# A linear-attention block gated by a Hadamard FFN: preparing work on VectorE handed out one operation at a time behind the reads of PSUM

## The chip, the cores and the metric

One Trainium2 chip, one core of it. The metric is device time of one execution in microseconds, the median of three runs. The profile is of one further execution of the same program.

## The reference

All data are fp32. Eight sequences of 512 tokens with 512 features are layer-normalised (without weights). From the normalised tokens two branches are computed and joined: an attention branch `s` and a gating branch `g`; the result is `x + s * silu(g)`. Cut to what matters:

```
xn = layernorm(x)                                   # (8, 512, 512)
q, k, v = xn @ Wq.T + bq, xn @ Wk.T + bk, xn @ Wv.T + bv
kv = cumsum((elu(k) + 1) * v, axis=tokens)
s  = ((elu(q) + 1) * kv * 32**-0.5) @ Wo.T + bo
h  = fwht(xn * SU_ug) / 64                          # Walsh-Hadamard, 512 wide
up, gate = h @ W_up.T * (.. * 64), h @ W_gate.T * (.. * 64)     # 2048 wide
y  = fwht(silu(gate) * up * SU_dp) / 64
g  = silu(y @ W_down.T * (Wscale_dp * 64))
out = x + s * g
```

## The kernel before

**Fast products.** Every matrix product is done with seven block products in place of eight. The blocks are called P1 to P7; tokens and weights are "encoded" into seven combinations each by additions, and the results are summed from three PSUM banks called px, py and pz (three, one and two buffers). `group` and `token_groups` run one such product with tokens on the moving or on the stationary side. What PE leaves in PSUM is read in two ways: snapshots of px by ACT (`snapshot`, `read`), and sums of a snapshot with py or pz by DVE (`output`, L343 in `group` and L418 in `token_groups`). A group has three such sums in `group` and six in `token_groups`. A bank is free for the next product when its sum has been read. In the output projection px is read by DVE too (L414).

**Pairs of sequences.** The sequences are handled in pairs p = 0 to 3. Attention of pair 0, attention of pair 1, the output projection of pair 0 within it, then the FFN of pair 1, then the FFN of pair 0, then pairs 2 and 3 whole. An attention is six groups (k, v, q, twice); the first FFN is sixteen groups of gate and up, and two of down.

**First-pass weights.** Weights are prepared once and kept in DRAM for the later pairs. The first FFN uses gate and up weights with the input's Hadamard transform folded in. `folded_w` makes one such weight in two steps: `butterflies` (four DVE operations, L777 to L780), then `fold` (two pairs of PE products with a Hadamard matrix, ACT copies, and four DVE encodings in `encode_weights`, L187 to L190). From two folded weights `inner_w` makes a second level of seven for the later pairs, with four DVE additions (L276 to L285) and DMA stores. The down weights get their Hadamard transform in `butterflies_down` (one multiplication L818, then for each half of the columns four stages of an addition L763 and a subtraction L764, so 17 instructions a tile), `fold_down` (PE, ACT, a store to `wd_f`) for each of four tiles, and are encoded by `down_w` in eight pieces. `layernorm` of the sequences 2 and 3 (L123 to L130) and their transposes by `transposed` run beside the first attention.

**What sets the order.** Two things. The program text puts PE's products in a hand-made order with `at(place, fn)` and `advance(n)`: a place is one block product, so the products of neighbouring groups interleave. Then a scheduler orders each engine's instructions by a simulation, among those ready by priority; `background(n)` gives the instructions traced within it a priority n behind. The order is fixed when the program is built. The down weights' steps are started by a table, `plan`, that says after how many groups each is traced, as a whole and in the background:

```
for o, (n, a, b) in enumerate(((1, 4, 6), (4, 7, 9), (7, 10, 12), (10, 13, 15))):
    plan.setdefault(n, []).append(lambda o=o: load_down(o, rs))
    plan.setdefault(a, []).append(lambda o=o: rd.update({o: butterflies_down(o, rs)}))
    plan.setdefault(b, []).append(lambda o=o: fold_down(o, rd[o]))
```

`between()`, called at the end of each group, runs what is due. The butterflies of folded weights are placed 12 places after they are asked for and their fold 6 later, both in the foreground. `get_w` fetches weights for three groups ahead. Weight tiles have four buffers ("w"), working tiles six ("t"), token inputs one ("x"). All these DMAs are issued on SP's queue.

Of the kernel before, what the change touches and what calls it, by code (L numbers as in the profile page):

```python
# [21 lines left out]
def kernel(  # L22
# [27 lines left out]
    nc = tc.nc  # L50
# [32 lines left out]

    cols_sb = const.tile([P, cols.shape[1]], F32, tag="cols", name="cols_sb")
# [13 lines left out]
    wsc_r = const.tile([P, P], F32, tag="wsc_r", name="wsc_r")  # L98
# [17 lines left out]

    def layernorm(b, xt, parts=1):
        n = NT // parts
        for i in range(0, NT, n):
            mv = small.tile([P, n, 2], F32, tag="mv", name=f"mv_{b}_{i}")  # L120
            for t in range(n):
                st = small.tile([P, 6], F32, tag="st", name=f"st_{b}_{i}_{t}")
                nc.vector.bn_stats(st, xt[:, i + t, :])  # L123
                nc.vector.bn_aggr(mv[:, t, :], st)
            rstd = small.tile([P, n], F32, tag="rstd", name=f"rstd_{b}_{i}")
            nc.vector.tensor_scalar(rstd, mv[:, :, 1], EPS, None, ALU.add)
            nc.scalar.activation(rstd, rstd, AF.Sqrt)
            nc.vector.reciprocal(rstd, rstd)
            for t in range(n):
                nc.vector.tensor_scalar(  # L130
                    xt[:, i + t, :], xt[:, i + t, :], mv[:, t, 0:1], rstd[:, t : t + 1],
                    ALU.subtract, ALU.mult,
                )
# [51 lines left out]
    def encode_weights(eng, w):  # L185
        w = w.rearrange("p j s e -> p s j e") if len(w.shape) == 4 else w
        eng.tensor_tensor(w[:, P5], w[:, P7], w[:, P4], ALU.add)  # L187
        eng.tensor_tensor(w[:, P6], w[:, P5], w[:, P1], ALU.subtract)  # L188
        eng.tensor_tensor(w[:, P3], w[:, P2], w[:, P6], ALU.subtract)
        eng.tensor_tensor(w[:, P7], w[:, P1], w[:, P7], ALU.subtract)  # L190

# [59 lines left out]
    def down_w(u, j):  # L251

        t = t8.tile([P, 2, 7, P], F32, tag="t", name=f"wd_{u}_{j}")
        w = by_factor(t)
        rows_w(w, wd_f, u + NU * j, NG)

        def encode():
            encode_weights(nc.vector, w)
            nc.sync.dma_start(wd[u // 2][:, :, 2 * (u % 2) + j], w)

        at(8, encode)

    def inner_w(m, u, w0, w1):

        if u not in inner:
            inner[u] = dram.tile([P, 7, 2, 7, P], F32, tag=f"d_gu_{u}", name=f"d_gu_{u}")
        d = inner[u][:, :, ("gate", "up").index(m)]

        def store(c, t):
            nc.sync.dma_start(d[:, :, c, :], t)  # L270

        store(P1, w0[:, 0])
        store(P2, w0[:, 1])
        store(P4, w1[:, 1])
        t = xin.tile([P, 3, 7, P], F32, tag="x", name=f"s_{m}_{u}")
        nc.vector.tensor_tensor(t[:, 0], w1[:, 0], w1[:, 1], ALU.add)  # L276
        store(P5, t[:, 0])
        nc.vector.tensor_tensor(t[:, 1], t[:, 0], w0[:, 0], ALU.subtract)
        store(P6, t[:, 1])
        nc.vector.tensor_tensor(t[:, 2], w0[:, 1], t[:, 1], ALU.subtract)  # L280
        store(P3, t[:, 2])

        def s3():
            with background():
                nc.vector.tensor_tensor(t[:, 0], w0[:, 0], w1[:, 0], ALU.subtract)  # L285
                store(P7, t[:, 0])

        at(7, s3)
# [27 lines left out]
    def group(name, ws, rhs, dst, at_x, then, bias=(None, None)):  # L316
# [25 lines left out]
        def output(i, s, p):  # L342
            nc.vector.tensor_tensor(dst[i], s, p.rearrange("p a t -> p (a t)"), ALU.add)  # L343
# [41 lines left out]
        between()  # L385


    def token_groups(name, n, tok, wts, dst, add=None, early=None, done=None):
# [28 lines left out]
        def output(o, p, a, s, g):  # L417
            nc.vector.tensor_tensor(dst(a, s, g), o, p, ALU.add)  # L418
            if done:
                done(a, s, g)  # L420
# [55 lines left out]
        between()  # L476
# [64 lines left out]
    def attention(p, xo, get_w, behind):  # L541
# [4 lines left out]
        def project(m, g, then):  # L546
            w = get_w(m, g)
            r = t8.tile([P, 2, 2, L], F32, tag="t", name=f"{m}_{p}_{g}")
            b = (col("b" + m, g), col("b" + m, g + 2))

            def whole(px):
                nc.scalar.activation(r[:, 0, 1], px, AF.Identity, bias=b[0])  # L552

            group(
                f"{m}_{p}_{g}", [w[:, 0], w[:, 1]], x_rhs(xo),
                (r[:, 0, 0], r[:, 1, 0], r[:, 1, 1]), whole, lambda: then(r), b,
            )
            behind.get(next(n), lambda: None)()
# [56 lines left out]
    def project_out(p, co, get_w):  # L615
        ws = [get_w("o", k) for k in range(2)]
        r = [t8.tile([P, NT, D], F32, tag="t", name=f"o_{p}_{s}") for s in range(2)]

        def bias(a, s, g):
            return bo_r[:, a * 2 * P : (a + 1) * 2 * P].unsqueeze(1).to_broadcast([P, 2, 2 * P])  # L620

        token_groups(
            f"o_{p}", 2, lambda k, i: co[:, k, i, :], lambda i: lambda k: ws[k][:, i],
            lambda a, s, g: block(r[s], a, g), bias,
        )
        for s in range(2):
            put_by(f"s_{p}_{s}", r[s])


    def gate(p, f, xo, get_w):  # L630
# [6 lines left out]
        def with_gate():  # L637
# [5 lines left out]
            (g[:, 0, 0], g[:, 1, 0], g[:, 1, 1]), at_x, with_gate,  # L643
# [3 lines left out]
    def up(p, f, g, xo, ho, get_w):  # L647
# [7 lines left out]
        def with_up():  # L655
# [6 lines left out]
            (r[:, 0, 0], r[:, 1, 0], r[:, 1, 1]), at_x, with_up,  # L662
# [58 lines left out]
    def down(p, half, hos, get_w, ds=None, ss=None, ys=None):  # L721
# [21 lines left out]
        def at_ds(a, s, g):  # L743
# [3 lines left out]
            f"dn_{p}_{half}", 4, lambda k, i: hos[k // 2][:, k % 2, i, :], wts, at_ds,  # L747
# [12 lines left out]
    def butterfly(eng, dst, src, h):  # L760
        s = src.rearrange("p (a t h) e -> p a t h e", t=2, h=h)
        d = dst.rearrange("p (a t h) e -> p a t h e", t=2, h=h)
        eng.tensor_tensor(d[:, :, 0], s[:, :, 0], s[:, :, 1], ALU.add)  # L763
        eng.tensor_tensor(d[:, :, 1], s[:, :, 0], s[:, :, 1], ALU.subtract)  # L764

    def folded_w(name, src, f):
# [3 lines left out]
        rs = []  # L770

        def butterflies():
# [4 lines left out]
            nc.vector.tensor_tensor(r2[:, 0], a, b, ALU.add)  # L777
            nc.vector.tensor_tensor(r2[:, 1], a, b, ALU.subtract)
            nc.vector.tensor_tensor(r[:, :, 0], r2[:, :, 0], r2[:, :, 1], ALU.add)
            nc.vector.tensor_tensor(r[:, :, 1], r2[:, :, 0], r2[:, :, 1], ALU.subtract)  # L780

        def fold():
            for b in range(2):
# [11 lines left out]
            encode_weights(nc.vector, w)  # L795
            folded[name, f] = w
            if f >= NU:
                with background():
                    inner_w(name, f - NU, folded[name, f - NU], w)

        return w, [(12, butterflies), (6, fold)]
# [4 lines left out]
    def down_tiles(rs):  # L806
        n = NF * P
        r = [rs[:, i * n : (i + 1) * n].rearrange("p (c e) -> p c e", c=NF) for i in range(2)]
        return r + [rs[:, 2 * n : 2 * n + n // 2].rearrange("p (c e) -> p c e", c=NF)]

    def load_down(o, rs):
        r = rs[o % 2]
        nc.sync.dma_start(r, wdown_t[:, o * P : (o + 1) * P].rearrange("(c p) e -> p c e", p=P))
        nc.sync.dma_start(wsc_r, wscale_dp[o * P : (o + 1) * P].partition_broadcast(P))

    def butterflies_down(o, rs):
        r, r2 = rs[o % 2], rs[2]
        nc.vector.tensor_tensor(r, r, wsc_r.unsqueeze(1).to_broadcast([P, NF, P]), ALU.mult)  # L818
        for e in range(2):
            half = r[:, :, e * P // 2 : (e + 1) * P // 2]  # L820
            butterfly(nc.vector, r2, half, 8)
            butterfly(nc.vector, half, r2, 4)
            butterfly(nc.vector, r2, half, 2)
            butterfly(nc.vector, half, r2, 1)
        return r
# [19 lines left out]
    def first_w(m, g):  # L845
# [18 lines left out]
        return w, [(5, encode)]  # L864

    def later_w(m, g):
        return stream_w((m, g)), []
# [32 lines left out]
    def ask(n):  # L900
        while queue and len(ahead) < n:
            first, m, g = queue.pop(0)
            w, steps = (first_w if first else later_w)(m, g)
            ahead.append({"key": (m, g), "w": w, "steps": steps, "traced": 0, "asked": 0, "place": 0})
# [8 lines left out]
    def get_w(m, g):  # L913
# [4 lines left out]
        for _ in e["steps"]:  # L918
            step_of(e)()
        for i, e in enumerate(ahead):  # L920
# [36 lines left out]
    rd = {}  # L957
    groups = [0]
    plan = {}
    for o, (n, a, b) in enumerate(((1, 4, 6), (4, 7, 9), (7, 10, 12), (10, 13, 15))):  # L960
        plan.setdefault(n, []).append(lambda o=o: load_down(o, rs))
        plan.setdefault(a, []).append(lambda o=o: rd.update({o: butterflies_down(o, rs)}))
        plan.setdefault(b, []).append(lambda o=o: fold_down(o, rd[o]))
    for n, u, j in ((16, 0, 0), (16, 0, 1), (17, 1, 0), (18, 1, 1), (22, 2, 0), (23, 2, 1), (24, 3, 0), (25, 3, 1)):
        plan.setdefault(n, []).append(lambda u=u, j=j: down_w(u, j))

    def between():
        for step in plan.pop(groups[0], []):
            with background():
                step()  # L970
        groups[0] += 1

    def tokens(b, xo):
        t = load_x(b)
        layernorm(b, t)
        transposed(b, t, xo)
# [63 lines left out]
    def next_tokens(b):  # L1040
        with background(40):
            tokens(b, x1)

    co0 = attention(0, x0, get_w, {0: lambda: next_tokens(2), 2: lambda: next_tokens(3), 4: put_x0})
    co1 = attention(1, x1, get_w, {1: lambda: project_out(0, co0, get_w)})
    ffn(1, x1, None, True, co1, {3: fetch_x0})
# [62 lines left out]
```

## Time and profile before

| | |
|---|---|
| median of 3 runs | 1607.16 us (1606.34 to 1608.49) |
| profiled execution | 1607.51 us, span 1605.7 us, mean granted PE clock 0.995 |
| PE busy | 1548.8 us (96% of the span), 5936 matmuls |
| DVE busy | 959.9 us (60%), 1385 instructions |
| ACT busy | 422.2 us (26%) |
| POOL busy | 494.1 us (31%) |
| DMA | 261.64 MB, mean 163 GB/s |

The span is the time from the first to the last instruction; the execution's own time holds a little more at both ends. Busy time counts instructions that run; matmuls are pipelined and their ends are modelled, so PE at 96% is not PE at its peak. In the chain of work that ended last PE has 76%, DVE 12%, POOL 5%. The rows of the timeline name the tile written and the tiles read: `q<-sb_q,pz_q` is the sum of the snapshot sb_q and the bank pz_q into q.

### The profile page before, as it was taken

The page shows a single profiled execution, that of the slowest core. Times are in us where ns is not written, and L with a number is a line of the kernel's source. Part 1 is how long each engine was busy: PE and PEld are TensorE (multiplying, and loading weights), DVE is VectorE, ACT ScalarE, POOL GpSimd, SP SyncE. Part 2 cuts the span into 40 slices and gives each one's busy share as a digit, 9 for nine tenths or more (in the row PEclk, how much of TensorE's full clock was granted, in tenths as well). Part 3 has the DMA queues.
Part 4 walks back from the last instruction along what each step waited for, and adds up shares of the span by engine and source line. Part 5 has one row for each costly group of instructions (what it writes and reads, how often), then busy time and mean ns, then how long its engine had stood idle before and what let it go on. Part 6 is the DMA issues. An engine that isn't in the chain of part 4 may idle for free.

```text
span 1605.7 us, 15724 instructions
## 1 busy us (share of the span) xinstructions
PE 1548.8 (96%) x5936; PEld 1114.4 (69%) x5936; DVE 959.9 (60%) x1385; ACT 422.2 (26%) x677; POOL 494.1 (31%) x286
## 2 busy tenths in 40 slices
PE   6898988999999999999999999999999999999998
PEld 3346435546744688888886468888887468888887
DVE  6896487582377566715684575634675376542673
ACT  2442444231233112111222431111221451111211
POOL 4343121223013425502622236201622128120731
PEclk9999999999999999999999999999999999999999
DMA  8512443684594864335563133525464133525462
GB/s 321 179 62 99 146 134 97 199 274 134 190 277 141 302 236 160 110 114 189 177 251 140 69 125 109 190 93 186 167 256 157 50 113 136 176 84 190 142 258 85
DMA packets 148876, 261.64 MB, mean 163 GB/s; under 512 B 7360, under 2 KB 109248, under 8 KB 144576
## 3 DMA queue, kind: packets, MB, share of 16 engines
q1 hardware_dynamic: 148512, 260.34, 48.0%
q8 instruction: 47, 0.77, 0.2%
q10 hardware_dynamic: 288, 0.30, 0.1%
q14 instruction: 29, 0.24, 0.0%
HBM read 187.20 MB, written 73.40 MB: 162 GB/s over the span
## 4 chain that ended last, share of the span: by engine, by line
PE 76%; DVE 12%; POOL 5%; issue 3%; ACT 2%; DMA 2%; POOLq 0%; SPq 0%; ACTq 0%; DVEq 0%
PE px_gu L487 17%; PE px_dn L403 9%; PE pz_gu L487 9%; PE pz_dn L403 5%; PE py_gu L487 4%; PE px_up L327 3%; PE px_gate L327 3%; PE px_o L403 3%; PE py_dn L403 3%; PE px_k L327 2%; PE px_v L327 2%; PE px_q L327 2%; POOL s L730 2%; PE pz_o L403 2%; PE pz_up L327 1%
## 5 line engine op out<-in xcount | busy, mean ns | idle before, releaser
L403 PE MATMUL px_dn<-w_down,ho 128*128 128x256 f32 x1024 | 229.7, 379 | 2.1 <-DVE sb_dn L414 1.1
L403 PEld LDWEIGHTS px_dn<-w_down,ho 128*128 128x128 f32 x1024 | 193.8, 190 | 31.8 <-DVE sb_dn L414 1.9
L487 PE MATMUL px_gu<-xi,w_gu 128*128 128x256 f32 x672 | 173.3, 380 | 1.2 <-ACT sa_gu L495 1.0
L487 PE MATMUL px_gu<-xo,w_gu 128*128 128x256 f32 x672 | 172.4, 379 | 0.0
L693 POOL TENSOR_TENSOR u<-u,v 128x1024 f32<-128x1024 f32 x24 | 56.2, 2364 | 328.2 <-DVE u L525 295.7
L487 PEld LDWEIGHTS px_gu<-xi,w_gu 128*128 128x128 f32 x672 | 126.9, 190 | 23.2 <-issue 2.4
L487 PEld LDWEIGHTS px_gu<-xo,w_gu 128*128 128x128 f32 x672 | 127.7, 190 | 18.2 <-issue 1.0
L403 PE MATMUL pz_dn<-w_down,ho 128*128 128x256 f32 x512 | 116.8, 380 | 4.0 <-POOL ho L182 4.0
L403 PEld LDWEIGHTS pz_dn<-w_down,ho 128*128 128x128 f32 x512 | 96.5, 190 | 20.1 <-POOL ho L182 4.8
L730 POOL TENSOR_TENSOR s<-s,d 128x512 f32<-128x512 f32 x30 | 41.4, 1379 | 165.0 <-ACT d L728 165.0
L487 PE MATMUL pz_gu<-xo,w_gu 128*128 128x256 f32 x336 | 86.8, 381 | 0.7 <-DVE v L343 0.7
L487 PE MATMUL pz_gu<-xi,w_gu 128*128 128x256 f32 x336 | 86.3, 379 | 0.0
L487 PE MATMUL py_gu<-xo,w_gu 128*128 128x256 f32 x336 | 86.2, 379 | 0.0
L577 POOL TENSOR_TENSOR v<-v,k 128x1024 f32<-128x1024 f32 x16 | 42.2, 2635 | 141.3 <-ACT v L552 90.7
L487 PEld LDWEIGHTS pz_gu<-xo,w_gu 128*128 128x128 f32 x336 | 63.3, 190 | 11.2 <-DVE v L343 1.5
L487 PEld LDWEIGHTS pz_gu<-xi,w_gu 128*128 128x128 f32 x336 | 63.8, 190 | 9.0 <-DVE u L518 0.4
L487 PEld LDWEIGHTS py_gu<-xo,w_gu 128*128 128x128 f32 x336 | 63.8, 190 | 8.7
L697 POOL TENSOR_TENSOR v<-v,r 128x1024 f32<-128x1024 f32 x24 | 56.2, 2362 | 25.6 <-DVE r L525 23.4
L327 PE MATMUL px_gate<-xo,w_gate 128*128 128x512 f32 x128 | 60.3, 599 | 3.7 <-DVE w_gate L188 3.7
L179 POOL TENSOR_TENSOR co<-co 128x512 f32<-128x512 f32 x8 | 15.3, 1918 | 156.9 <-DVE co L587 144.9
L327 PE MATMUL px_k<-xo,w_k 128*128 128x512 f32 x128 | 60.9, 594 | 1.7 <-ACT sa_k L339 1.7
L327 PE MATMUL px_q<-xo,w_q 128*128 128x512 f32 x128 | 61.5, 599 | 0.0
(245 smaller groups left out, 2687.3 us busy)
## 6 DMA issues: line engine op xcount, KB each, us to landing
w_gu<-d_gu SPq DMA_DIRECT2D x84, 896.0 KB, 4.4
w_down<-d_down SPq DMA_DIRECT2D x56, 512.0 KB, 3.4
d_s<-o SPq DMA_DIRECT2D x8, 1024.0 KB, 5.5
d_d<-dn SPq DMA_DIRECT2D x8, 1024.0 KB, 7.4
d<-d_d SPq DMA_DIRECT2D x8, 1024.0 KB, 5.4
s<-d_s SPq DMA_DIRECT2D x8, 1024.0 KB, 7.1
y<-in_x_dram SPq DMA_DIRECT2D x8, 1024.0 KB, 8.5
out_dram<-y SPq DMA_DIRECT2D x16, 512.0 KB, 3.1
```

The costliest lines, as they stand in the source:

```text
L179: eng.tensor_tensor(o[..., P5, :], o[..., P7, :], o[..., P1, :], ALU.subtract)
L327: nc.tensor.matmul(p.rearrange("p a t -> p (a t)") if len(r.shape) == 2 else p, ws[k][:, i, :], r, start=(first and k == 0), stop=(k == n ...
L403: nc.tensor.matmul(p[:, c], t[:, (2 * g + c) * P : (2 * g + c + 1) * P], ws[i](k), start=(first and k == 0 and c == 0), stop=(k == n - 1), ...
L487: nc.tensor.matmul(p[:, lane], w[:, lane, i, :], x(i), start=(first and lane == 0), stop=True, skip_group_check=True,)
L577: nc.gpsimd.tensor_tensor(v[:, h], v[:, h], k[:, h], ALU.mult)
L693: nc.gpsimd.tensor_tensor(r[:, m], ru1[:, m], rv[:, m], ALU.add)
L697: nc.gpsimd.tensor_tensor(rv[:, m], rv[:, m], rr[:, m], ALU.add)
L730: (nc.vector if last else nc.gpsimd).tensor_tensor(r, r, d, ALU.mult)
```

## The change

DVE's preparing operations are no longer traced as whole steps. Each becomes an entry of a list, with a cost in us that the author gives it, in one of two queues: `urgent` (butterflies, encodings and inner weights of gate and up) and `idle` (layernorm of sequences 2 and 3, the down weights' butterflies and encodings). Each sum at L343 and L418 calls `pace` with a budget `us`, and `pace` takes entries from `urgent`, then from `idle`, until the budget is used up. What an entry traces on DVE is queued behind that sum by `tc.issue_after` (an order of issue, without a wait for its end) and has background priority. The budgets are 2.0 in attention, 2.2 in the output projection, 3.2 in gate and up, 3.0 in down. `finish` runs at once what is left of a list when its result is wanted. The table `plan`, `between` and `butterflies_down` go. The operations themselves and their shapes stay, but for the multiplication L818, which is done in two halves, and the order of the four inner weights, which begins with P7. The scale vector of the down weights gets a second buffer; the first two down tiles are loaded after the first group, each further one after the fold two tiles before it. A fold of a down tile is placed 4 places after its last butterfly, in the foreground. The encodings of the down weights for the first half follow the last fold, those for the second half the group down_0.

```diff
+    urgent, idle = [], []
+    def run(step):
+        fn, step[1] = step[1], None
+        if fn:
+            fn()
+    def finish(steps):
+        for step in steps:
+            run(step)
+    def pace(ins, us):
+        while us > 0 and (urgent or idle):
+            step = (urgent or idle).pop(0)
+            if step[1]:
+                with tc.issue_after(ins.ins), background():
+                    run(step)
+                us -= step[0]
...
+    def layernorm_steps(b, xt, tiles=range(NT)):
...
+        return steps_of(
+            *[(0.8, lambda i=i: stats(i)) for i in range(n)], (0.2, root),
+            *[(0.6, lambda i=i: scaled(i)) for i in range(n)],
+        )
...
+    def encode_steps(w):
...
+            *[(0.42, lambda a=a, b=b, c=c, op=op: nc.vector.tensor_tensor(w[:, a], w[:, b], w[:, c], op))
...
     def down_w(u, j):
-        def encode():
-            encode_weights(nc.vector, w)
+        def kept():
             nc.sync.dma_start(wd[u // 2][:, :, 2 * (u % 2) + j], w)
-        at(8, encode)
+        return encode_steps(w) + steps_of((0, kept))
...
     def inner_w(m, u, w0, w1):
...
+        return steps_of(
+            (1.1, lambda: factor(P7, 0, lambda t: w0[:, 0], lambda t: w1[:, 0], ALU.subtract)),
+            (1.1, lambda: factor(P5, 1, lambda t: w1[:, 0], lambda t: w1[:, 1], ALU.add)),
+            (1.1, lambda: factor(P6, 2, lambda t: t[:, 1], lambda t: w0[:, 0], ALU.subtract)),
+            (1.1, lambda: factor(P3, 0, lambda t: w0[:, 1], lambda t: t[:, 2], ALU.subtract)),
+        )
...
         def output(i, s, p):
-            nc.vector.tensor_tensor(dst[i], s, p.rearrange("p a t -> p (a t)"), ALU.add)
+            pace(nc.vector.tensor_tensor(dst[i], s, p.rearrange("p a t -> p (a t)"), ALU.add), us)
...
         advance(7 * u)
-        between()
...
     def folded_w(name, src, f):
         def butterflies():
...
+            rs.extend(steps_of(*[
+                (0.68, lambda x=x: nc.vector.tensor_tensor(*x)) for x in (
...
+            urgent.extend(rs[1:])
         def fold():
+            finish(rs[1:])
...
-            encode_weights(nc.vector, w)
+            enc.extend(encode_steps(w))
+            urgent.extend(enc)
             folded[name, f] = w
             if f >= NU:
-                with background():
-                    inner_w(name, f - NU, folded[name, f - NU], w)
-        return w, [(12, butterflies), (6, fold)]
+                urgent.append([0, lambda: urgent.extend(inner_w(name, f - NU, folded[name, f - NU], w))])
+        return w, [(10, butterflies), (5, fold)], enc
...
+    def down_steps(o, rs):
...
+        def folded():
+            fold_down(o, r)
+            if o + 2 < KD:
+                load_down(o + 2, rs)
+            if o == KD - 1:
+                prepare_down(0)
+        return steps_of(
+            *[(1.2 if op[3] == ALU.mult else 0.68, lambda op=op: nc.vector.tensor_tensor(*op)) for op in ops],
+            (0, lambda: at(4, folded)),
+        )
...
     def later_w(m, g):
-        return stream_w((m, g)), []
+        if m == "down":
+            while not ready[g[0]]:
+                run(idle.pop(0))
+        return stream_w((m, g)), [], []
...
     def get_w(m, g):
...
         for _ in e["steps"]:
             step_of(e)()
+        finish(e["last"])
...
+    def begin(n):
+        if n == 0:
+            next_tokens(2)
+            for o in range(2):
+                load_down(o, rs)
+            for o in range(KD):
+                idle.extend(down_steps(o, rs))
+        elif n == 2:
+            finish(held[2])
+            next_tokens(3)
+        elif n == 4:
+            put_x0()
...
-    ffn(1, x1, None, True, co1, {3: fetch_x0})
+    ffn(1, x1, None, True, co1, {1: lambda: prepare_down(1), 3: fetch_x0})
+    finish(urgent + idle)
```

## The prediction

> **What bounds the kernel now.** I read the page first (the busy rows in forty slices), then the busy time of each engine by stages, then what TensorE waited for in the disturbed stretch, then the timeline of DVE at the longest of these waits. The page:
>
> ```profile
> span 1605.7 us, 15724 instructions
> ...
> PE   6898988999999999999999999999999999999998
> ...
> DVE  6896487582377566715684575634675376542673
> ```
>
> PE stands at 9 from slice 9 on; what it loses it loses before 320 us, where DVE swings between 2 and 9. Columns of the next view: stretch, its length, then busy us of PE, PEld, DVE, ACT, POOL, granted clock, DMA.
>
> ```profile
> 40.00:80.00 40.00, 34.76 (x91) 15.48 (x90) 33.17 (x39) 17.11 (x22) 14.51 (x10) 0.97 0.57 179
> 80.00:120.00 40.00, 39.16 (x98) 17.22 (x97) 37.58 (x53) 18.66 (x26) 17.08 (x10) 0.95 0.18 60
> 120.00:160.00 40.00, 34.22 (x132) 24.34 (x131) 27.11 (x31) 8.65 (x10) 15.28 (x10) 1.00 0.27 96
> 160.00:200.00 40.00, 40.00 (x96) 17.92 (x96) 15.94 (x17) 18.66 (x34) 5.73 (x3) 1.00 0.47 153
> 200.00:240.00 40.00, 32.58 (x74) 13.18 (x73) 32.91 (x39) 16.16 (x36) 8.80 (x4) 1.00 0.43 134
> 240.00:280.00 40.00, 33.16 (x101) 19.85 (x100) 29.68 (x44) 17.35 (x32) 6.35 (x4) 0.91 0.33 98
> 320.00:360.00 40.00, 40.00 (x95) 17.76 (x94) 33.87 (x57) 13.74 (x26) 9.04 (x6) 1.00 0.88 279
> ```
>
> DVE is full in 40 to 120, nearly idle in 160 to 200 and loaded again in 200 to 280. The preparing work comes in lumps. At 320 to 360 a DVE load of 34 of 40 us costs PE nothing, so the load as such is bearable where it is spread. PE's waits from 30 to 310 us:
>
> ```profile
> PE pz_v L327 <- DVE rstd L126: 5.0, 1, 5.0
> PE pwd L831 <- ACT rd L837: 3.9, 3, 3.2
> PE px_gate L327 <- DVE w_gate L188: 3.7, 1, 3.7
> PE pz_q L327 <- DVE q L343: 2.5, 1, 2.5
> PE pz_o L403 <- POOL co L182: 2.4, 1, 2.4
> PE pz_v L327 <- DVE q L343: 2.3, 1, 2.3
> ```
>
> With the smaller ones (1.6, 1.2, 1.0, 0.9, 0.8, 0.7, 0.2) they make 26.2 us. The reduced clock adds 0.03 x 40 + 0.05 x 40 + 0.09 x 40 = 6.8 us. So 33.0 us are lost here. I sort them: 11.5 before 125 us (5.0 + 2.3 + 1.0 and 3.2 of clock); 3.3 in the first output projection at 130 to 155 (1.6 + 0.9 + 0.8), where DVE runs next to no preparing work; 18.2 from 200 to 310. How a wait comes about is seen in DVE's timeline at the first:
>
> ```profile
> 61.63 2.83 DVE L764 TENSOR_TENSOR rd<-rd 128x512 f32<-128x512 f32 x1
> 64.39 2.81 DVE L579 TENSOR_TENSOR_SCAN k<-ones,v 128x512 f32<-128x512 f32 x2
> 67.13 1.15 DVE L763 TENSOR_TENSOR rd<-rd 128x512 f32<-128x512 f32 x1
> 68.20 1.21 DVE L764 TENSOR_TENSOR rd<-rd 128x512 f32<-128x512 f32 x1
> 69.34 2.81 DVE L818 TENSOR_TENSOR rd<-rd,wsc_r 128x2048 f32<-128x2048 f32 x1
> ...
> 77.71 0.67 DVE L343 TENSOR_TENSOR q<-sb_q,pz_q 128x512 f32<-128x512 f32 x1
> ```
>
> From 61 to 77.7 us eight-odd preparing operations on rd and x stand ahead of the reads at L343. The read of pz_q ends at 78.4, and the next product into a pz bank starts at 78.52. No wait was missed by DVE: it is behind with its queue.
>
> **The change, part by part.** The operations stay the same ones: butterflies (L777 to 780), encodings (L187 to 190), inner weights (L276 to 285), layernorm (L123 to 130), the down weights' butterflies (L763, L764, L818). What changes is their place. Each is now queued behind one read at L343 or L418, 2.0 us of them per read in attention, 2.2 in the output projection, 3.2 in gate and up, 3.0 in down.
>
> Attention first. The queue called idle holds two layernorms, each 4 x 0.69 + 0.3 + 4 x 0.5 = 5.1 us, and four down tiles, each 16 adds at 0.605 (start to start) and two half-size multiplications at 1.15 (half of L818's 2.29), 12.0 us: 58 us in all. The transposed tokens' own DVE work adds 6 (the L157 to L162 rows of 40 to 120). At 2.0 us of budget a read takes three adds, so a tile takes six reads and both layernorms seven: 31 reads. Three come per group of attention and six in the output projection, so idle lasts about ten group lengths from 32 us on. A group is 28 matmuls at 0.43 = 12.0 us of PE, so with the transposes this is 124 us of PE work. DVE's own part there is 5.7 us a group (in 40 to 120, five groups: 15 reads x 0.6, 8 scans x 1.2, 8 operations L565 and L587 x 1.21), nine times, and 14 reads x 0.6 of the projection: 59.
>
> **A rule against the change.** The row: L764 at 61.63 takes 2.83 us where 0.68 is usual, while POOL's L577 runs from 61.19 to 63.92. In 40 to 120 the excess over the usual durations is 5.3 (L764), 1.0 (L763), 1.1 (L818), 2.5 (L579), 0.9 (L130), 10.8 us in 80, against POOL's 31.6 busy. The Trainium skill (SBUF — State Buffer, SBUF: two separate sides) says that VectorE with two SBUF inputs and GpSimd take the shared ports as an exclusive lock for a whole instruction. A step between two reads that meets a POOL operation would then hold the next read for all of it, and spreading the steps makes such meetings likelier. By the trace's share, 0.135 x 124 = 16 us, demand on DVE is 59 + 64 + 16 = 139. By the rule at its worst, all of POOL's 46.9 us in 40 to 160, scaled to 48, demand is 171. I take the trace's 16, since it was measured at the same density of steps. The overrun is 139 - 124, less some 4 us that PSUM's banks absorb (the same sum for the old order in 54 to 125 gives 28 + 36 + 11 = 75 in 71 us elapsed): 11 us of PE waiting, where 11.5 + 3.3 = 14.8 were lost. Gain 3.8. So the lumps go, but the average stays near full.
>
> After attention. Before, two down tiles (24 us) lay in DVE's 62.6 busy us of 200 to 280; they are now done by about 165 us, and 38 of 80 us remain. Gone are then most of the pz_q waits (3.2), the px_gate wait (an encoding behind eight adds of rd, 3.7), the pwd wait (ACT waited for a late g, 3.9 and 0.2), the output projection's waits (2.4 and 1.2, late L587) and 3.6 of clock: 18.2. I leave 4 us of it for what the POOL collisions and the folds still cost. Gain 14.2.
>
> On the clock, the row: after the 5.0 us wait, four pz_v matmuls take 3.75 us where 1.88 is usual. The skill (TensorE: Matmul & The Clock Gate, Part 1) lets an idle window of about 3.4 us halve the clock. Here a 3.2 us wait at 240 also cost clock, so the measurement decides. Counting waits alone the part within reach is 22.9 us, with the clock 29.7. I use the latter. Waits split into pieces under 2 us, as the pace leaves them, kept 1.00 in 120 to 160.
>
> Costed at nothing, with the cover named:
> - Two loads of 1 MB (load_down 0 and 1, before at 45.8 and 55.7 us) move ahead to about 22 us on SP's queue, past the weight loads. The next weight load issues at 43.84, waiting for a buffer, so 20 us cover 2 x 6.6 (the landing seen at 231). Without cover up to 13.
> - The folds move with their tile's last step, four matmuls and sixteen ACT copies each, now in the foreground, and with them the stores to wd_f and the loads of tiles 2 and 3, which wait on SP for those stores. Before, DVE waited 2.0 for such a load. Between a gain of 4 and a loss of 5 I take 0, near the row at 168 to 179, four folds with no PE wait.
> - The four first down_w come earlier and each holds one of six "t" buffers from load to store. Before, four did so at 300 to 330 with no PE wait: 0, at worst 2.5 each, 10.
> - Inner weights begin with P7, and P3 waits for P7's store (before, DVE waited 3.4 once for it, no PE wait): 0, at worst 8 x 2.
> - The queue called urgent: a folded weight needs four butterflies at 0.68 and four encodings at 0.42, 4.4 us, every second one also four inner weights at 1.09, 8.8; the budget of a gate or up group is 3 x 3.2 = 9.6, so it drains: 0. That the encodings lose their foreground place is rival 3.
> - The Sqrt between layernorm steps: before 3.5 us passed from L126 to L128 with reads in between: 0.
>
> After 320 us PE has almost no waits and the DVE load is the old one: 0. Sum: 1607.51 (the profiled execution; span 1605.7, 1.8 around it, and 0.35 above the median) - 3.8 - 14.2 = 1589.5; I say 1590.
>
> **The rivals.**
> 1. All waits in reach go: no overrun, since DVE begins at 32 us rather than 54. 29.7 us less, 1578. For it: 160 to 200 was nearly empty. Against: the 139 above.
> 2. The ports decide, slower. Place: 32 to 165 us, POOL's L577 and its encodings against tied steps. At the full 48 us the overrun is 171 - 124 - 4 = 43 instead of 14.8, +28, less 14.2: 1621. It becomes slower when collisions pass 34 us, 70% of POOL's time instead of the 34% seen. Against it: that share was measured with DVE full.
> 3. Weights come late, slower. A background encoding waits for a read to pass before PE may use the weight; the row is px_gate's 3.7 us. At eight of the sixteen folded weights it is 30 us: 1619; from five on (18 / 3.7) the gain is gone. Against: the steps are first in line and are finished when the weight is fetched.
> 4. The edges bind little. They only set an earliest place; the scheduler may pile steps up later as before, and 40 to 120 and 200 to 280 stay full: 1604, gain of the earlier start alone.
>
> **How the numbers follow.** A run here can tell 0.2%, 3.2 us, from no change. Likeliest case 0.48 (its own range 1581 to 1599), rival 1 0.10, rival 2 0.12, rival 3 0.14, rival 4 0.16. Faster: 0.48 + 0.10 + half of rival 4, 0.08 = 0.66. Same: the other 0.08 of rival 4 and 0.04 of rivals 2 and 3 in mild form, 0.12. Slower: 0.22. The range 1577 to 1615 leaves out about half of rivals 2 and 3 above and a little of rival 1 below.
>
> **What would show it.** Right: DVE's digits level between 32 and 320 us, rd's adds done by about 170, no wait of PE over 3 us there, clock 1.00 from 40 on. The three reads' gaps hold at most three adds. Wrong: waits of PE for L343 adding to over 20 us in 32 to 165 (rival 2, with L763 and L764 means over 1 us), for w_gate or w_up (rival 3), or DVE's order unchanged (rival 4).

## The result: slower by half a per cent, and the profile after

Measured beside the kernel before: 1615.33 us (median of 4, 1614.76 to 1616.48) against 1607.36 us, a ratio of 1.005 with a 95% interval from 1.0033 to 1.0068. The forecast was 1590 us, with a range from 1577 to 1615. The page of the changed kernel, the rows that were shown of before (PE is TensorE, PEld its weight loads, DVE VectorE, ACT ScalarE, POOL GpSimd):

```profile
span 1613.7 us, 15738 instructions
...
PE   6988999999999999999999999999999999999998
...
DVE  5899666561467376625675476634675376552673
```

At this grain little has changed. The stages show more (columns as before: stretch, length, busy PE, PEld, DVE, ACT, POOL, granted clock, DMA share, GB/s):

```profile
40.00:80.00 40.00, 37.05 (x107) 18.00 (x106) 33.56 (x59) 20.06 (x29) 13.29 (x10) 0.96 0.53 189
80.00:120.00 40.00, 34.84 (x77) 15.09 (x76) 38.21 (x40) 16.90 (x33) 14.92 (x8) 0.91 0.27 81
120.00:160.00 40.00, 34.70 (x108) 21.04 (x107) 36.10 (x43) 15.38 (x29) 20.32 (x12) 0.96 0.45 150
160.00:200.00 40.00, 37.80 (x112) 20.73 (x111) 27.72 (x44) 12.72 (x38) 2.74 (x1) 1.00 0.68 231
200.00:240.00 40.00, 38.20 (x89) 16.48 (x89) 27.63 (x35) 20.87 (x30) 12.50 (x6) 1.00 0.48 156
240.00:280.00 40.00, 39.98 (x138) 25.64 (x137) 25.73 (x37) 14.80 (x19) 5.92 (x4) 1.00 0.43 122
...
400.00:440.00 40.00, 36.69 (x125) 23.86 (x124) 13.88 (x26) 8.77 (x17) 0.00 (x0) 0.96 0.43 136
...
480.00:520.00 40.00, 32.81 (x69) 13.96 (x69) 31.35 (x36) 11.05 (x22) 15.19 (x9) 0.91 0.50 150
```

Behind 160 us the load of DVE is levelled as intended: 27.7 in 160 to 200 where 15.9 stood, 25.7 in 240 to 280 where 29.7 stood, and PE loses next to nothing from 240 to 280. From 120 to 160 it rose, to 36.1 of 40 us where 27.1 stood. And there are two new holes in PE's work, at 400 to 440 and 480 to 520, in a stage where PE had been full. In the first of them DVE is at 13.9 of 40 us, which is no overload.

Lines of the changed kernel: the sums that read PSUM are L386 and L460 (L343 and L418 before), the butterflies of gate and up L813, their encodings L231, the inner weights L322, the down weights' butterflies L880, layernorm's last step L158. PE's waits by what they waited for, first from 30 to 330 us, then from 320 to 620, the largest of each:

```profile
PE pwd L898 <- DVE rd L880: 5.2, 1, 5.2
PE pt L184 <- DVE x L158: 3.0, 1, 3.0
PE py_o L445 <- DVE o L460: 2.4, 1, 2.4
PE pwd L898 <- issue: 2.0, 1, 2.0
PE pw_gate L826 <- DVE r_gate L813: 1.8, 1, 1.8
PE pwd L898 <- ACT rd L904: 1.7, 1, 1.7
```

```profile
PE pw_gate L826 <- DVE r_gate L813: 6.5, 2, 3.3
PE px_gate L370 <- DVE w_gate L231: 4.0, 1, 4.0
PE pz_dn L445 <- POOL ho L217: 3.2, 2, 1.6
PE pw_up L826 <- DVE r_up L813: 2.1, 2, 1.4
```

The attention products' waits for banks of PSUM (pz_v, pz_q, pz_k before) are gone; in the output projection py_o still waits 2.4 us for its bank. PE now waits mostly in its small products, the Hadamard folds pwd, pw_gate, pw_up and the transposes pt, and for the most part for paced steps; once, at px_gate, it waits for a paced encoding. Adding up each whole list (and the reduced clock, 40 us times what is missing to 1.00 in each stretch) gives the balance:

| PE's waits + clock, us | before | after |
|---|---|---|
| 30 to 320 us | 26.4 + 6.8 | 17.5 + 6.8 |
| 320 to 620 us | 5.3 + 0 | 17.6 + 5.2 |

So 8.9 us are gained and 17.5 lost, 8.6 net, against 8.0 between the spans (1613.7 and 1605.7).

### The profile page after: what moved, and what is told of

Its sections match the earlier page's. It is cut to its first block, busy times and chain, and to the rows that moved or that the text cites. A ratio compares the mean times of both kernels' runs of the same rounds, so it can differ in the third digit from the quotient of the medians.

```text
span 1613.7 us, 15738 instructions
## 1 busy us (share of the span) xinstructions
PE 1554.1 (96%) x5936; PEld 1118.5 (69%) x5936; DVE 949.3 (59%) x1389; ACT 421.5 (26%) x677; POOL 506.1 (31%) x286
## 4 chain that ended last, share of the span: by engine, by line
PE 75%; DVE 13%; POOL 4%; issue 3%; ACT 3%; DMA 2%; SPq 0%; POOLq 0%; DVEq 0%; ACTq 0%
PE px_gu L528 17%; PE px_dn L445 9%; PE pz_gu L528 9%; PE pz_dn L445 4%; PE py_gu L528 4%; PE px_gate L370 3%; PE px_o L445 3%; PE py_dn L445 3%; PE px_k L370 2%; PE px_up L370 2%; PE px_v L370 2%; PE px_q L370 2%; DVE rd L880 2%; POOL s L771 2%; PE pz_o L445 2%
## 5 line engine op out<-in xcount | busy, mean ns | idle before, releaser
L528 PEld LDWEIGHTS px_gu<-xo,w_gu 128*128 128x128 f32 x672 | 127.7, 190 | 18.2 <-issue 1.0
L697 POOL TENSOR_TENSOR ho<-g,u 128x512 f32<-128x512 f32 x8 | 16.0, 2002 | 164.0 <-DVE u L386 164.0
L880 DVE TENSOR_TENSOR rd<-rd 128x512 f32<-128x512 f32 (+1 forms) x72 | 63.0, 898 | 0.6
L214 POOL TENSOR_TENSOR co<-co 128x512 f32<-128x512 f32 x8 | 18.6, 2324 | 141.7 <-DVE co L628 141.7
```

The lines of the kernel that those rows point to most:

```text
L214: eng.tensor_tensor(o[..., P5, :], o[..., P7, :], o[..., P1, :], ALU.subtract)
L528: nc.tensor.matmul(p[:, lane], w[:, lane, i, :], x(i), start=(first and lane == 0), stop=True, skip_group_check=True,)
L697: nc.gpsimd.tensor_tensor(ho[:, P1], g[:, 0, 0], r[:, 0, 0], ALU.mult)
L880: *[(1.2 if op[3] == ALU.mult else 0.68, lambda op=op: nc.vector.tensor_tensor(*op)) for op in ops],
```

## The experiments

Two theories. A step is tied when it is queued behind a read by `tc.issue_after`. Theory 1: a tied step cannot run until its read has run; where that read comes late, and the product that needs the step stands right behind in PE's queue, PE waits for read and steps together. Theory 2: DVE is simply slower or fuller with the steps spread, by POOL's hold on the ports or by load.

What the first hole looks like in DVE's timeline of the changed kernel, with PE's below it:

```profile
402.05 0.69 DVE L460 TENSOR_TENSOR dn<-sc_dn,pz_dn 128x512 f32<-128x512 f32 x1 [6.77 <-ACT sc_dn L454]
405.50 0.69 DVE L460 TENSOR_TENSOR dn<-sc_dn,pz_dn 128x512 f32<-128x512 f32 x1 [2.76 <-ACT sc_dn L454]
415.24 0.69 DVE L460 TENSOR_TENSOR dn<-sb_dn,pz_dn 128x512 f32<-128x512 f32 x1 [9.05 <-PE pz_dn L445]
418.69 0.69 DVE L460 TENSOR_TENSOR dn<-sb_dn,pz_dn 128x512 f32<-128x512 f32 x1 [2.76 <-PE pz_dn L445]
419.30 1.29 DVE L813 TENSOR_TENSOR r_gate<-w_gate 128x512 f32<-128x512 f32 x2
420.62 1.29 DVE L813 TENSOR_TENSOR r_gate<-r_gate 128x512 f32<-128x512 f32 x2
```

```profile
411.59 7.07 PE L445 MATMUL pz_dn<-w_down,ho 128*128 128x256 f32 x32
421.97 3.17 PE L826 MATMUL pw_gate<-r_gate,had 128*128 128x512 f32 x4 [3.31 <-DVE r_gate L813]
424.93 2.44 PE L370 MATMUL px_gate<-xo,w_gate 128*128 128x512 f32 x4
```

DVE idles 9.05 us, then 2.76, and only behind the last read of the down group come the four butterflies, 2.6 us. PE's next product in line is the one that needs them: read 0.6 and butterflies 2.6 are the 3.3 us of the wait. The row of pw_gate shows a second price: its four products take 3.17 us where 1.88 is usual; the granted clock of 400 to 440 is 0.96, which is 1.6 us.

The second hole looks different:

```profile
478.99 2.57 DVE L322 TENSOR_TENSOR s_up<-w_up,w_up 128x896 f32<-128x896 f32 x1
481.49 1.74 DVE L813 TENSOR_TENSOR r_gate<-r_gate 128x512 f32<-128x512 f32 x1
...
485.24 3.42 DVE L813 TENSOR_TENSOR r_gate<-w_gate 128x512 f32<-128x512 f32 x2
488.58 2.57 DVE L231 TENSOR_TENSOR w_gate<-w_gate 128x256 f32<-128x256 f32 x1
```

```profile
483.28 3.04 PE L826 MATMUL pw_gate<-r_gate,had 128*128 128x512 f32 x4 [3.22 <-DVE r_gate L813]
...
494.36 3.62 PE L370 MATMUL px_gate<-xo,w_gate 128*128 128x512 f32 x4 [3.97 <-DVE w_gate L231]
```

From 475.4 to 498 us DVE works without a pause. The last of four butterflies stands behind three reads and two inner weights, the encoding behind the next weight's butterflies; beside POOL's operations an inner weight takes 2.57 us where 1.09 is usual, a butterfly 1.74 where 0.68 is, an encoding 2.57 where 0.42 is. That is a full queue with slowed operations, as theory 2 has it. This hole is the larger one: 3.2 + 4.0 us of waits and 3.6 of clock, against 3.3 + 1.6 of the first.

### a1: the butterflies of gate and up free again

```diff
-            urgent.extend(rs[1:])
+            finish(rs[1:])
```

> The changed kernel, but the four butterflies of each folded gate or up weight are issued at once where they are asked for (not behind a read, foreground), as before the change. Theory 1 (a Hadamard product stands in PE's queue before its butterflies, which are held back behind a late read): PE's waits for r_gate and r_up, 10.4 us together, go, and with them the 5.2 us of reduced clock between 400 and 520 us and most of the 4.0 us wait for w_gate; about 1600 us (1597 to 1604). Theory 2 (DVE is slower as a whole there, by POOL's port or by load, whatever the order): the waits turn up at other reads, 1611 to 1616.

Measured 1598.81 us, ratio to before 0.9953 (0.994 to 0.9965), 16.5 us under the changed kernel. In the same place DVE now does:

```profile
401.86 0.69 DVE L460 TENSOR_TENSOR dn<-sc_dn,pz_dn 128x512 f32<-128x512 f32 x1 [6.77 <-ACT sc_dn L454]
402.46 1.29 DVE L813 TENSOR_TENSOR r_gate<-w_gate 128x512 f32<-128x512 f32 x2
403.78 1.29 DVE L813 TENSOR_TENSOR r_gate<-r_gate 128x512 f32<-128x512 f32 x2
...
415.05 0.69 DVE L460 TENSOR_TENSOR dn<-sb_dn,pz_dn 128x512 f32<-128x512 f32 x1 [3.74 <-PE pz_dn L445]
418.50 0.69 DVE L460 TENSOR_TENSOR dn<-sb_dn,pz_dn 128x512 f32<-128x512 f32 x1 [2.77 <-PE pz_dn L445]
```

```profile
411.40 7.07 PE L445 MATMUL pz_dn<-w_down,ho 128*128 128x256 f32 x32
418.31 1.88 PE L826 MATMUL pw_gate<-r_gate,had 128*128 128x512 f32 x4
```

The butterflies ran some 17 us earlier, in time in which DVE had nothing else, and pw_gate follows at once at its usual pace. From 320 to 620 us PE's waits are 5.2 us, about the 5.3 of before, and no clock is lost: both holes are gone. At the place of the second, DVE's operations are as slow as they were (at 494.79 us two butterflies take 3.42), but they run ahead of need and PE does not wait. Theory 1 forecast the size; under theory 2 the waits would have turned up at other reads, and they did not. Before 320 us the waits are the 17.5 of the changed kernel. The edit lifts the tie and the background priority together; a2 and b2 take these apart.

### a4: half of the change, layernorm and the down weights alone

```diff
-            urgent.extend(rs[1:])
+            finish(rs[1:])
...
-            enc.extend(encode_steps(w))
-            urgent.extend(enc)
+            encode_weights(nc.vector, w)
...
-                urgent.append([0, lambda: urgent.extend(inner_w(name, f - NU, folded[name, f - NU], w))])
+                with background():
+                    finish(inner_w(name, f - NU, folded[name, f - NU], w))
-        return w, [(10, butterflies), (5, fold)], enc
+        return w, [(12, butterflies), (6, fold)], enc
```

> Half of the change: layernorm and the down weights are paced behind reads, gate and up weights (butterflies, encodings, inner weights) are treated as before the change. Theory 1 says that all loss after 320 us comes from the half left out: after 320 us the kernel loses no more than before the change, and before 320 us it keeps the 8.7 us gained; 1597 to 1602. Theory 2: the paced half fills DVE in attention, no gain: 1606 to 1610.

Measured 1598.02 us, ratio 0.9955 (0.9941 to 0.9968): within the runs of a1. So of the gate and up weights it is the pacing of the butterflies that costs; whether their encodings and inner weights are paced is worth nothing here.

### a2: the steps traced at the same reads, without the tie

```diff
-                with tc.issue_after(ins.ins), background():
+                with background():
```

> The changed kernel without the tie: steps are traced one by one at the same reads and in the background, but the scheduler may issue them ahead of the read. Theory 1: the wait of 3.3 us at 420 us, where DVE idles 9 us ahead of the read, goes, and part of the others; 1603 to 1610. If instead the late place in the text and the background priority do the harm and the tie nothing, or under theory 2: 1613 to 1617.

Measured 1605.95 us, ratio 0.9997 (0.9988 to 1.0005). From 320 to 620 us PE waits 5.4 us in place of 17.6 and loses 1.6 us of clock in place of 5.2; from 30 to 320 it waits 23.0 in place of 17.5 and loses 10.4 us of clock in place of 6.8, with the old sort of wait again (`pz_k` for `v`, 4.6 us in one piece). One edge has both effects: it protects the reads in attention and delays the butterflies later.

### b2: tied, but not in the background

```diff
+            behind = 0 if urgent else 150
             step = (urgent or idle).pop(0)
             if step[1]:
-                with tc.issue_after(ins.ins), background():
+                with tc.issue_after(ins.ins), background(behind):
```

> The changed kernel with the steps of gate and up weights still tied behind reads, but without the background priority (those of layernorm and the down weights keep it). If the tie itself is the cause, the late read stands ahead of the butterflies as before and the 3.3 us waits at the Hadamard products stay: 1610 to 1616. If the low priority is the cause, they go: 1598 to 1604.

Measured 1614.85 us, ratio 1.0046 (1.0034 to 1.0059). PE waits 10.5 us for r_gate in the whole run. The priority is not the cause; with a2 this leaves the tie.

### c2: tied, but asked for earlier

```diff
-        return w, [(10, butterflies), (5, fold)], enc
+        return w, [(2, butterflies), (5, fold)], enc
```

> The changed kernel, everything tied as it is, but the butterflies of a folded weight are asked for 2 places ahead and not 10, so that more reads lie between them and their Hadamard product. If it is the lateness of the read that counts (product close behind the last read), PE's waits for r_gate and r_up fall from 10.4 to under 4 us: 1602 to 1608. If a tie hurts wherever it stands, or DVE then waits for the weight's DMA instead: 1612 to 1618.

Measured 1605.95 us, ratio 0.9999 (0.999 to 1.0007). Between 320 and 620 us no wait for r_gate or r_up is left. A tie does no harm here, where reads enough lie between the step and its product:

```profile
424.25 0.69 DVE L460 TENSOR_TENSOR dn<-sb_dn,pz_dn 128x512 f32<-128x512 f32 x1 [9.06 <-PE pz_dn L445]
424.85 1.28 DVE L813 TENSOR_TENSOR r_gate<-w_gate 128x512 f32<-128x512 f32 x2
426.17 1.29 DVE L813 TENSOR_TENSOR r_gate<-r_gate 128x512 f32<-128x512 f32 x2
427.70 0.69 DVE L460 TENSOR_TENSOR dn<-sb_dn,pz_dn 128x512 f32<-128x512 f32 x1 [0.24 <-PE pz_dn L445]
```

In these rows the next gate weight's butterflies hang on the read before the last, not on the last. That the whole is not as fast as a1 comes from before 320 us: one new wait of 6.5 us of px_gate for w_gate, at 238 us, and 12.0 us of clock in place of 8.4.

### b1: the other half, gate and up weights alone

The kernel before, with `pace`, the budgets, the paced `folded_w` and `inner_w`, and `finish(e["last"])` in `get_w`; layernorm and the down weights' table `plan` as they were.

> The other half of the change: the kernel before, with only the gate and up weights (butterflies, encodings, inner weights) paced behind reads; layernorm and the down weights stay as they were. If the two halves simply add, this loses 43 us before 320 us as before the change and some 27 from 320 to 620 us as after it (7.5 before): 1607 + 19 = 1626 us (1620 to 1630). If the loss of the gate and up weights only comes about together with the other half: 1605 to 1612.

Measured 1616.52 us, ratio 1.0057 (1.0043 to 1.0071). The sign is as forecast and the size is half. PE's waits from 320 to 620 us are 14.7, with 9.7 for r_gate and r_up in the whole run, but the second hole of the changed kernel (480 to 500 us) is missing. So tied butterflies cost 9.4 us there without it. Nor do the halves add up: a4 gains 8.5 us and b1 loses 9.2, 0.7 together, where the whole change loses 8.0. The second hole, 10.8 us with its clock, is of the size of the difference. Why inner weights, butterflies and encodings meet there in the changed kernel and not in b1 is not shown.

### b3 and c3: a smaller budget in attention

```diff
-                (r[:, 0, 0], r[:, 1, 0], r[:, 1, 1]), whole, lambda: then(r), 2.0, b,
+                (r[:, 0, 0], r[:, 1, 0], r[:, 1, 1]), whole, lambda: then(r), 1.3, b,
```

b3 has it on top of a1, c3 on the changed kernel.

> As a1 (butterflies of folded weights free), with the budget in attention at 1.3 us a read, two additions instead of three; the rest of the steps then falls to the output projection and the gate groups. If DVE is overrun in attention, PE's waits between 60 and 185 us for x, rd, o and ACT's rd (15 us with the clock) shrink by more than half: 1588 to 1594. If these waits come from where the small products stand, not from the load: 1597 to 1602.

Measured 1592.10 us, ratio 0.9906 (0.9892 to 0.9919), the fastest kernel of the study that does the whole computation: 15 us under before, 6.7 under a1. The waits of pwd for rd and of pt for x that the changed kernel had in attention are not in its list; at 40 to 80 us PE loses nothing. What is new in its place:

```profile
PE px_o L445 <- DVE co L628: 3.4, 1, 3.4
...
PE pz_k L370 <- DVE v L386: 3.2, 1, 3.2
```

Up to 185 us b3 loses 7.4 us in waits and 1.6 of clock, where a1 has 15.6 and 6.8. So in attention the load per read was too high at 2.0 us. Of these 13.4 us about half is paid back from 185 to 320 us, where b3 loses 10.6 us and a1 3.5.

> The changed kernel with nothing but the budget in attention at 1.3 us a read in place of 2.0. If the overrun in attention and the late butterflies are two separate losses, this gains what b3 gained over a1, 6 to 8 us: 1607 to 1610, about the kernel before. If the steps put off then collide with the tied butterflies of the gate groups: 1612 to 1620.

Measured 1612.41 us, ratio 1.0034 (1.0021 to 1.0046). It gains 2.9 us on the changed kernel, not 6 to 8. Its waits for r_gate and r_up rise from 10.4 to 17.6 us: probably the steps that attention no longer takes stand in the gate groups' way, where the butterflies are still tied.

### b4: less work for POOL in attention

```diff
-            encode_weights(eng, w)
+            v = w.rearrange("p j s e -> p s j e") if len(w.shape) == 4 else w
+            for s in (P5, P6, P3):
+                nc.scalar.copy(v[:, s], v[:, P1])
```

> As a1, with the four additions that POOL makes on each of the eight first-pass weights of q, k, v and o left out (three copies on ACT instead, with other values), some 40 us less of POOL in the first 140 us. If POOL's hold on the ports lengthens DVE's steps and so makes PE's waits in attention, the loss before 320 us falls from 33 to 24 to 28 us: 1590 to 1594. If it hardly matters: 1597 to 1600.

This kernel leaves out additions that the result needs and computes other values; it serves for its time alone. Measured 1589.22 us, ratio 0.9889 (0.9876 to 0.9903): just under the range for the ports. But the rows do not carry the reason. In 30 to 130 us the down weights' additions take 0.804 us a piece where a1 has 0.850, less than 2 us over 37 of them, and the multiplications got longer (1.65 where 1.32). The gain must lie mostly elsewhere: POOL's encodings also stand between the first weights and PE, and in the first 320 us PE is busy 293.7 us against 290.0. The edit changed two things at once, and how much the ports cost is not settled by it.

### a3, d1, d2: the small products later in the text

a3 makes both edits on the changed kernel, d1 the first, d2 the second.

```diff
-            (0, lambda: at(4, folded)),
+            (0, lambda: at(12, folded)),
...
-        return layernorm_steps(b, t) + steps_of((0, lambda: at(0, lambda: transposed(b, t, xo))))
+        return layernorm_steps(b, t) + steps_of((0, lambda: at(6, lambda: transposed(b, t, xo))))
```

> The changed kernel with the fold of a down tile placed 12 places after its last butterfly (4 before) and the transposes 6 places after the last layernorm step (0 before). Theory 1 (PE's small products come too soon behind steps that are still queued): PE's waits for rd (5.2 and 2.0, 1.7 on ACT) and x (3.0) go, with some 5 us of reduced clock from 65 to 120 us; 1602 to 1608. Theory 2 (DVE is overrun in attention and PE must wait somewhere): the same time is lost at reads of pz and py, 1612 to 1616.

> The changed kernel with only the fold of a down tile 12 places behind its last butterfly in place of 4. If the fold stands too early, its 5.2 us wait at 98 us goes with the clock: 1606 to 1610. If DVE is overrun there (as the smaller budget suggested), the time is lost in part at the next read: 1611 to 1616. In a3 this edit stood together with the next one, which came out 8 us slower.

> The changed kernel with only the transposes 6 places behind the last layernorm step in place of 0. If this edit made a3 slow (DVE's 6 us of foreground work on the transposed tokens then meets the co operations, and the output projection waits 7 us for its sums): 1620 to 1625. If not, the 3.0 us wait and its clock go: 1609 to 1613.

Measured 1623.78 us, ratio 1.011 (1.0096 to 1.0124); d1 1625.37, ratio 1.0116 (1.0101 to 1.013); d2 1614.66, ratio 1.0047 (1.0035 to 1.0059). None came out in either range that it was given. The expectation of d2 laid a3's loss on the transposes; it is d1 that has it. In d1 the fold did not move in PE's queue at all. The changed kernel first, then d1:

```profile
97.08 1.88 PE L370 MATMUL py_k<-xo,w_k 128*128 128x512 f32 x4
104.12 3.78 PE L898 MATMUL pwd<-rd,had 128*128 128x512 f32 x4 [5.16 <-DVE rd L880]
```

```profile
96.52 1.88 PE L370 MATMUL py_k<-xo,w_k 128*128 128x512 f32 x4
103.55 3.78 PE L898 MATMUL pwd<-rd,had 128*128 128x512 f32 x4 [5.16 <-DVE rd L880]
```

The same 5.16 us at the same place: the place in the text is not what put it there. (In a3 and d2, whose transposes come later, this wait is 3.2 us.) What did move is the load of tile 2 behind the fold; DVE then waits 1.81 us for it at 127 us, and PE 7.4 us at 138 for a read, behind these steps. In d2 the 3.0 us wait of pt for x is gone, and two waits of pt for xo, 1.8 us together, came in its place. These runs do not carry theory 1 over to attention; the budget of b3 does better there.

### c1 and d3: two more candidates

c1 lowers the budgets of b3 further: 2.0 in gate and up, 1.3 in the output projection. d3 is a4 with 1.3 in attention.

> As b3 (butterflies of folded weights free, 1.3 us a read in attention), with the output projection at 1.3 and gate and up at 2.0 us a read as well. b3 still loses 8 us at 240 to 280, where the rest of the down tiles fell to the first gate groups. If too much work per read is the rule there too, these shrink to 3: 1586 to 1590. If the steps only move on to later groups and delay the encodings: 1591 to 1597.

> As a4 (only layernorm and down weights paced), with 1.3 us a read in attention. The two gains, free gate and up weights and less per read, are those of b3, so 1590 to 1594; if foreground encodings crowd the first gate groups where the last down tiles now fall: 1595 to 1600.

Measured 1601.35 us, ratio 0.9962 (0.995 to 0.9975), and 1605.44 us, ratio 0.9998 (0.999 to 1.0005). Both are slower than either range that they were given. c1 has waits of 4.3 us for r_gate and 2.2 for w_up (0.4 and none in b3), and 3.6 of pz_o for g (0.8 in b3); the steps seem only to have moved on. d3 waits 10.5 us in one piece in the output projection for co, and 4.4 for g. With the order of everything set by one list, a change of 0.7 us in a budget moves single waits of 3 to 10 us about; b3 is the best of the points tried, not a rule.

## Why the prediction was wrong

**The failed step.** The line that costs the queue called urgent at nothing ("so it drains: 0"), and with it "After 320 us ... 0". By its sum the work does fit the budgets (8.8 of 9.6 us a group). What was not asked is when the last step is done, counted from the product that needs it. The waits for r_gate, r_up and w_gate from 320 to 620 us are 12.6 us, and with the 5.2 us of clock they are the whole loss there. That it comes from tying the butterflies, and so late, is shown: it goes when they are free (a1), when the tie alone is dropped (a2) and when they are asked for earlier (c2), and stays without the low priority (b2). How it comes about is plain only in the first hole, 4.9 us with its clock: a late read. In the second, 10.8 us, a full queue of DVE and operations slowed beside POOL take part; what each of them adds is open. Rival 3 had the mechanism of weights that come late, but put it at px_gate waiting for an encoding; that occurred once (4.0 us), and the other waits were one stage earlier, at the Hadamard products. It was given 0.14.

**The premise behind it.** The prediction used the full slices of 320 to 360 as proof that a spread load is harmless. There the butterflies were free to run whenever DVE was idle, and a1 shows that this is what counted: with 31.3 of 40 us of DVE load in that slice, and its butterflies free, PE is full. The change took that freedom away while the work stayed.

**Attention, a term of the wrong size and sign.** The overrun of DVE was forecast as 11 us of PE waiting, a gain of 3.8. Up to 185 us the changed kernel's waits are 15.7 (5.2 + 3.0 + 2.4 + 2.0 + 1.7 + 1.2 + 0.2), and 6.8 us of clock come on top, which the sum left out on the ground that waits would come in pieces under 2 us. Three did not: 2.4, 3.0 and 5.2. That makes 22.5 us where 14.8 were lost before, a loss of 7.7. Two terms of the demand were also rounded down (59.7 to 59 and 16.7 to 16), 1.4 us together. The steps did not spread as counted either: between the reads at 111.8 and 122.0 us stand six additions on rd, not three at most, and the last addition is done at 181.6 us, not by 170. b3 shows that the load per read was indeed the cause of most of it.

**What was right.** The waits from 200 to 310 us, 18.2 us with their clock, were to shrink to 4; 1.8 us are left, a gain of 16.4 where 14.2 was forecast. In all: 7.7 lost, 16.4 gained, 17.5 lost, 8.8 net, where the forecast had 3.8 gained, 14.2 gained, 0. The bank waits before 125 us are gone. DVE's digits are nearly level from 160 to 320 us (6 6 6 5 where 4 8 7 5 stood), but not before. Half of the change alone (a4) gives a gain of 8.5 us, though less than the 18 forecast. Rival 2, the ports, does not show its signs in attention: PE's waits for the sums there are 1.2 and 2.4 us and not over 20, and an addition on rd took 0.84 us on the mean from 40 to 160 us where the kernel before had 0.88. Of the two estimates of the ports that the prediction weighed, the smaller seems the better one. What share the ports still have in attention's loss is left open by b4.

**On the clock.** One wait of the changed kernel, and one of the kernel before:

```profile
152.12 2.98 PE L445 MATMUL py_o<-w_o,co 128*128 128x256 f32 x8 [2.39 <-DVE o L460]
```

```profile
229.39 1.96 PE L327 MATMUL px_gate<-xo,w_gate 128*128 128x512 f32 x4 [3.66 <-DVE w_gate L188]
```

After the wait of 2.39 us eight products took 2.98 us where 1.89 is usual, and the granted clock from 152 to 157 us was 0.66. After the wait of 2.95 us (pt at 70 us) four products of pz_q took 2.46 us where 1.88 is usual. After the wait of 3.66 us in the kernel before nothing was lost: the clock of 200 to 240 is 1.00. So here the length of a wait alone does not say whether it costs clock; where it did after the two shorter waits, the price was 1.6 us (0.04 x 40) on top of the wait. The Trainium skill (TensorE: Matmul & The Clock Gate, Part 1) speaks of an idle window of about 3.4 us; in this trace less was enough, and the measurement decides.

## What to carry to other kernels

Tying background work to an engine's reads sets an earliest time for it; before doing so, find for each step the instruction that consumes it, and count the reads that lie between. A step whose consumer stands right behind the last read belongs ahead of that read, or free. In this kernel levelling the engine's load gained what its lumps cost, but only for work without a near deadline, and with a budget that left the engine below its limit with everything else it had in that stage.

## What the runs showed of the hardware

The tie itself cost no time on DVE: the tied butterflies start 0.61 us after the start of their read (418.69 to 419.30 us), the free ones of a1 0.60 us (401.86 to 402.46). An addition of two SBUF tensors took up to 2.83 us beside a POOL operation in the kernel before and up to 2.72 us in the changed one (at 113 us), 0.68 alone. So splitting work into single operations does not keep a read from standing behind a long one: ahead of the read at 483.15 us stand an inner weight of 2.57 us and a butterfly of 1.74.
